# A gated graph network and a graph attention layer on one core: the weights of the beginning in a new order, two products of the end moved

## The chip, the cores and the metric

The kernel runs on one core of a Trainium2 chip. The metric is the device time of one execution in microseconds (us), lower is better. The core has five engines that run instruction streams of their own: TensorE (PE in the profile; its weight loads are listed apart as PEld), VectorE (DVE), ScalarE (ACT), GpSimd (POOL) and SyncE (SP). SyncE here only starts transfers; GpSimd starts those that add to what they find.

## The reference

The inputs are `x` (64 graphs, 256 nodes, 256 values, f32) and `adj` (64 x 256 x 256, zeros and ones, about one in 64 set). Two layers, each added to `x`:

```python
# layer 0: three steps of a gated graph network
h = relu(layernorm(x));  A = (adj != 0)
for l in range(3):
    m    = h @ weight[l]
    aggr = einsum('bst,bsd->btd', A, m)
    gi, gh = aggr @ w_ih.T + b_ih, h @ w_hh.T + b_hh       # 768 values each: r, z, n
    r = sigmoid(i_r + h_r); z = sigmoid(i_z + h_z)
    n = tanh(i_n + r * h_n)
    h = (1 - z) * n + z * h
x = x + h
# layer 1: graph attention, 4 heads of 64
v = relu(layernorm(x)) @ W.T + b
logits = leaky_relu(l_src[i] + l_dst[j], 0.2)              # l_src, l_dst: v times halves of a, per head
logits = where(adj == 1, logits, -9e15)
x = x + softmax(logits, over j) @ v
```

The message weights and the gates' input weights are multiplied into one another before use: the kernel needs `weight[l] @ w_ih.T` for each step, called `w_a[l]` here, with some sums and differences of its blocks.

## The kernel before

**Tiles.** The 64 graphs go through in 32 pairs, numbered 0 to 31. A pair has 512 nodes, four blocks of 128 rows. Layer 0 keeps the state turned (`hT_a`: values across partitions, nodes along the free axis), two halves of 512 elements; each graph of the pair is one half's inner part. A product of a step is a `block` (L302; its matmul is L313): four matmuls of 128x128 by 128x256 into one PSUM bank. The profile shows every f32 matmul as two, so a block as eight and the two small `pa` products of `value_weights` as four. The aggregation (`pa`, L470) works with the state in two parts, `hNhi` and `hNlo`, whose sum is the state and which are multiplied with `edge`, the adjacency as 0 and 1.

**Order.** Everything is entered in a plan: `at(tick, phase, p, fn)`. Ticks are run in order, the phases STEP, READY and REST within a tick, and of several pairs the later one first. The instructions are issued to the engines' streams in just that order (`tc.manual_schedule`), and each engine keeps it. Pair p starts at tick 18p. Its step l takes the ticks 12l to 12l+5 (`tick_0` to `tick_5`), `update` makes the new state in tick 12l+6, and the state is turned back to rows (`back`, PSUM bank `pback`) in ticks 12l+7 and 12l+8, where ScalarE copies `hNhi` (L798) and VectorE takes the difference `hNlo` (L799). Six ticks without a step follow each step; in them the next or the previous pair has a step of its own. So two pairs in different steps share TensorE, with the attention of earlier pairs between. Only at the two ends is there nothing to share with.

**Banks and buffers.** The steps' products have five PSUM banks of their own (`gate_bank`). All else, transposes and small products too, takes one of three banks in turn through `bank(name)`; a request waits until the bank's last reader is done. SBUF tiles have a tag with a fixed number of buffers: four of `zz` (logits later, weights as loaded at the beginning), two of `o`, two of `noedge`.

**The beginning.** Pair 0 has no neighbour, and its ticks 6 to 11 and 18 to 23 are partly filled with the weights, which are entered at the end of the program (L1018 to L1033):

- `biases` and `state_weights` at tick -5: the latter turns `w_hh` (banks `pw_hh`, copies to `hh_T` on ScalarE) and then issues six ScalarE operations for `w_n` and `w_h`. `state_weights_2` at -2 makes sums of them on VectorE.
- `first_hi` and `first_lo` of pair 0 (the two parts of its first state, L787 and after) at tick -3, `to_edge` (L764) at -2.5. The two halves of `hT_a` of pair 0 are turned at ticks -4 and -3.
- `input_weights` at tick 0 turns `w_ih` and the first message weights. `step_weights_T(l)` turns `weight[l]` (bank `pmT`), and ScalarE copies it to `w_msgT` (L232). `step_weights(l)` has four banks `pc_l` of two matmuls each, 128x128 by 128x384 (L239, four in the profile), copies each to `w_a[l]`, by VectorE and ScalarE in turn (L243), and after each two makes four sums S1, S2, S4 and -ZA of blocks on VectorE. The calls stand at ticks 0 and 1 for l = 0, 5 and 6 for l = 1, 13 and 14 for l = 2.
- `value_weights` at tick 20 prepares `w_val` (W turned, and behind it eight columns of W times the attention vectors) and `b_val`: a memset, then for each half two transposes (`pwv`, L280), a VectorE copy, two matmuls with 8 columns (`pwa`), a copy, and in the end the same for the bias (`bmat`, `pb`).

**Layer 1 of a pair.** From about tick 32 of the pair on: normalization, `values` (bank `pv`), `score_rows` (`as_rows`, L893: the scores are turned in bank `pscore`, written to DRAM as rows and read back for all partitions as `drow`), logits `zz` in which GpSimd's transfers add the score rows, maxima over the neighbours on VectorE (L949, reading `drow` and `noedge`), the shift `topT` written to DRAM and added to `zz` by GpSimd's transfers in the same way, exponentials (ScalarE), and for each block of rows `product` (bank `po`, 8 matmuls, 16 in the profile) with `divided`: VectorE's reciprocal `rden` and product `o` (L584), GpSimd's addition to `x` (L589). Pairs up to 28 enter a block's `output` at ticks 62 to 65 of the pair; for pairs below 29 (`dma_b`) `later` is six ticks, so that pair 28's last product stands at tick 71 of that pair.

**The end.** The last pair, 31, has its attention in `plan_tail` in a form without DRAM rows. From the end of its third step on, the order is a list written out by hand, `order` (L725), which mixes in what is left of pairs 29 and 30: `do("product", 2, r)` is the product of block r of pair 29, `do("rows", 1)` turns the maxima of pair 30 (`ptopT`, L887). The mask `noedge` of pair 31 is made by `bar` (L839 and around) at tick 28 of that pair.

Of the kernel before, what the change touches and what calls it, by code (L numbers as in the profile page):

```python
# [18 lines left out]
P = 128  # L19
# [8 lines left out]
def gated_gnn_then_gat_kernel(  # L28
# [51 lines left out]
    S0 = H * VC  # L80
    VW = S0 + 2 * H
    NPAIR = B // PB
# [15 lines left out]
    def bank(name):  # L98
        return ps_m.tile([P, 512], F32, tag="mm", name=name)
# [5 lines left out]
    def buf(tag, shape, name, dtype=F32):  # L105
        return sb.tile(shape, dtype, tag=tag, name=name, bufs=BUFS.get(tag, 1))
# [41 lines left out]
    w_nat = load_square("zz", "w_nat", W)  # L148
# [6 lines left out]
    ident = const.tile([P, P], F32, name="ident")  # L155
# [7 lines left out]
    for i in range(GB):  # L163
        pt = gate_bank(f"fill_{i}")
# [11 lines left out]
    def turn_gates(name, nat, dst, evict):  # L176
        for k in range(KD):
            for g0 in range(0, G, 3):
                pt = bank(f"pw_{name}_{k}_{g0}")
                for g in range(3):  # L180
                    nc.tensor.transpose(pt[:, ts(g, P)], nat[:, g0 + g, ts(k, P)], ident)
                evict[g0 // 3](dst[k][:, g0 * P : (g0 + 3) * P], pt[:, : 3 * P])
# [20 lines left out]
    RA, ZA, NA, S1, S2, S4 = range(6)  # L203
    def state_weights():
        turn_gates("hh", hh_nat, hh_T, (nc.scalar.copy, nc.scalar.copy))
        for k in range(KD):
            r_, z_, n_ = (hh_T[k][:, ts(g, D)] for g in range(3))
            nc.scalar.mul(w_n[:, (N00, N01)[k], :], n_[:, :P], 0.5)
            nc.scalar.mul(w_n[:, (NS3, N11)[k], :], n_[:, P:], 0.5)
            nc.scalar.copy(w_h[:, k, ts(RH, D)], r_)  # L210
# [13 lines left out]
    def step_weights_T(l):  # L224
        w_msgT[l] = buf("zz", [P, KD, D], f"w_msgT_{l}")
        pt = bank(f"pmT_{l}")
        for e in range(KD):
            for k in range(KD):
                nc.tensor.transpose(
                    pt[:, e * D + k * P : e * D + (k + 1) * P], w_msgs[l][:, k, ts(e, P)], ident  # L230
                )
        nc.scalar.copy(w_msgT[l].rearrange("q e d -> q (e d)"), pt)  # L232

    def step_weights(l):
        for k in range(KD):
            for g0 in range(0, G, 3):
                pt = bank(f"pc_{l}_{k}_{g0}")
                for e in range(KD):
                    nc.tensor.matmul(  # L239
                        pt[:, : 3 * P], w_msgT[l][:, e, ts(k, P)], ih_T[e][:, g0 * P : (g0 + 3) * P],  # L240
                        start=(e == 0), stop=(e == KD - 1),
                    )
                (nc.scalar.copy if g0 else nc.vector.tensor_copy)(  # L243
                    w_a[l][:, k, g0 * P : (g0 + 3) * P], pt[:, : 3 * P]
                )
            blk = [w_a[l][:, k, ts(j, D)] for j in range(6)]
            nc.vector.tensor_add(blk[S1], hh_T[k][:, D : 2 * D], blk[ZA])  # L247
            nc.vector.tensor_sub(blk[S2], blk[S1], hh_T[k][:, :D])
            nc.vector.tensor_sub(blk[S4], blk[RA], blk[S2])
            nc.vector.tensor_scalar_mul(blk[ZA], blk[ZA], -1.0)  # L250

    w_val = const.tile([P, KD, VW], F32, name="w_val")
    b_val = const.tile([P, VW], F32, name="b_val")

    a_exp = const.tile([P, KD, 2 * H], F32, name="a_exp")
# [5 lines left out]
    def load_vectors():  # L261
# [10 lines left out]
            bass.AP(tensor=b.tensor, offset=b.offset, ap=[[0, P], [C, H], [1, C]]),  # L272
        )

    def value_weights():
        nc.vector.memset(w_val, 0.0)
        for k in range(KD):
            pt = bank(f"pwv_{k}")
            for g in range(KD):
                nc.tensor.transpose(pt[:, ts(g, P)], w_nat[:, g, ts(k, P)], ident)  # L280
            nc.vector.tensor_copy(
                w_val[:, k, :S0].rearrange("q (h c) -> q h c", h=H)[:, :, :C],
                pt[:, :D].rearrange("q (h c) -> q h c", h=H),
            )
            pa = bank(f"pwa_{k}")
            for g in range(KD):
                nc.tensor.matmul(
                    pa[:, : 2 * H], w_nat[:, g, ts(k, P)], a_exp[:, g, :],
                    start=(g == 0), stop=(g == KD - 1),
                )  # L290
            nc.vector.tensor_copy(w_val[:, k, S0:], pa[:, : 2 * H])
        bmat = buf("o", [P, KD, P], "bmat")
        pb = bank("pb")
        for k in range(KD):
            nc.vector.tensor_copy(bmat[:, k, :], bcol[:, k : k + 1].to_broadcast([P, P]))
        for k in range(KD):
            nc.tensor.matmul(
                pb[:, : 2 * H], bmat[:, k, :], a_exp[:, k, :], start=(k == 0), stop=(k == KD - 1)
            )
        nc.vector.tensor_copy(b_val[:, S0:], pb[:, : 2 * H])  # L300


    def flat(y):
# [23 lines left out]
    def at(tick, phase, p, fn):  # L327
        plan.setdefault(tick, ([], [], []))[phase].append((-p, fn))
# [265 lines left out]
    def plan_tail(t0, p, v, g, turn_back, residual):  # L594
# [126 lines left out]
        def do(what, q, *key):  # L721
            return left[what, p - q, *key]

        at(t0 + 28, REST, p, links)
        order = (  # L725
            lambda: g.update(0), do("rows", 1), do("product", 2, 0), lambda: turn_back(0), lambda: g.update(1),
            do("product", 2, 1), lambda: residual(0), lambda: stats(0), do("add", 1), lambda: turn_back(1),
            do("product", 2, 2), lambda: residual(1), lambda: result(0), lambda: turned(0), lambda: stats(1),
            do("product", 2, 3), do("divided", 2, 0), lambda: values(0), lambda: result(1), lambda: turned(1),
# [11 lines left out]
    def plan_pair(p):  # L741
# [5 lines left out]
        def ready(t, fn):  # L747
            at(t0 + t, READY, p, fn)
# [4 lines left out]
        def rest(t, fn):  # L753
            at(t0 + t, REST, p, fn)
# [12 lines left out]
        dma_a = p >= 2  # L767
        norm_ticks = (-14, -13, -13, -10) if dma_a else (-14, -13, -13, -7)
        xn_a = plan_norm(lambda: v["x"], f"a{p}", p, [t0 + t for t in norm_ticks])
        ready(-1 if p else -2.5, to_edge)  # L770
        if dma_a:
            ready(-9.5, lambda: nc.scalar.activation(flat(xn_a["xn"]), flat(xn_a["xn"]), AF.Relu))
            h = plan_turn(lambda: xn_a["xn"], "hT_a", f"a{p}", p, [t0 - 9, t0 - 8, t0 - 3])
# [9 lines left out]
            hi, lo = map(flat, v["hN"])  # L783
            nc.vector.scalar_tensor_tensor(lo, flat(xn_a["xn"]), 0.0, hi, op0=ALU.max, op1=ALU.subtract)

        ready(-3, first_hi)
        rest(-3, first_lo)  # L787

        def back(l, i):

# [50 lines left out]
                nc.sync.dma_start(v["noedge_rows"].rearrange("r q t -> q r t"), v["noedge"])  # L841

        rest(16 if last else 22, load_adj_1)
        ready(28 if last else 35, bar)
        if last:
            plan_tail(t0, p, v, g, lambda i: turn_back(L - 1, i), residual)
            return
# [156 lines left out]
        if p >= NPAIR - 3:  # L1004
            for r in range(R):
                left["product", p, r] = lambda r=r: product(p, r, logits[r // KN], v, bank if late else gate_bank)
                left["divided", p, r] = lambda r=r: divided(p, r, v, nc.gpsimd.tensor_add)
            left["write", p] = lambda: write(p, v["x"], 0, R)
        else:
            for r, t in enumerate((62, 63, 64, 65)):  # L1010
                rest(t + later, output(r))
            rest(66 + later, lambda: write(p, v["x"], 0, R))

# [3 lines left out]

    at(-5, READY, 0, biases)  # L1018
    at(-5, REST, 0, state_weights)
    at(-2, READY, 0, state_weights_2)  # L1020

    def input_weights():
# [3 lines left out]
    at(0, REST, 0, input_weights)  # L1026
    at(1, REST, 0, lambda: step_weights(0))
    at(2, REST, 0, load_vectors)
    at(5, REST, 0, lambda: step_weights_T(1))
    at(SUB, REST, 0, lambda: step_weights(1))  # L1030
    at(13, REST, 0, lambda: step_weights_T(2))
    at(14, REST, 0, lambda: step_weights(2))
    at(20, REST, 0, value_weights)  # L1033
    for tick in sorted(plan):
        for phase in plan[tick]:
# [32 lines left out]
```

## Time and profile before

| quantity | value |
|---|---|
| median of three runs | 2495.89 us (2495.83 to 2496.14) |
| profiled execution, its own time | 2498.09 us |
| its span (first to last instruction) | 2496.3 us |
| mean granted TensorE clock | 0.997 of full |
| TensorE busy | 2464.2 us, 99% of the span |
| VectorE busy | 1992.2 us, 80% |
| ScalarE busy | 1437.5 us, 58% |
| GpSimd busy | 494.3 us, 20% |
| memory traffic (HBM) over the span | 109 GB/s |
| instructions | 37566 |
| chain that ended last, by engine | PE 83%, DVE 12%, ACT 3% |

Durations and busy times come from one profiled execution; it took 2.2 us more than the median of the runs without a profile, and its span is 1.8 us shorter than its own time. A line number such as L313 is a line of the kernel before. `out<-in` names the tiles that an instruction writes and reads. In a list of waits, `A L1 <- B L2: 2.8, 2, 1.5` says that instructions of tile A at line 1 were held up by those of tile B at line 2, for 2.8 us in all, 2 times, 1.5 us at most. The granted clock is the share of full speed at which TensorE ran. A busy share of 99% does not say that TensorE runs at its peak: a matmul counts as busy at a lower clock as well.

### The profile page before, as it was taken

The page shows a single profiled execution, that of the slowest core. Times are in us where ns is not written, and L with a number is a line of the kernel's source. Part 1 is how long each engine was busy: PE and PEld are TensorE (multiplying, and loading weights), DVE is VectorE, ACT ScalarE, POOL GpSimd, SP SyncE. Part 2 cuts the span into 40 slices and gives each one's busy share as a digit, 9 for nine tenths or more (in the row PEclk, how much of TensorE's full clock was granted, in tenths as well). Part 3 has the DMA queues.
Part 4 walks back from the last instruction along what each step waited for, and adds up shares of the span by engine and source line. Part 5 has one row for each costly group of instructions (what it writes and reads, how often), then busy time and mean ns, then how long its engine had stood idle before and what let it go on. Part 6 is the DMA issues. An engine that isn't in the chain of part 4 may idle for free.

```text
span 2496.3 us, 37566 instructions
## 1 busy us (share of the span) xinstructions
PE 2464.2 (99%) x13446; PEld 2191.9 (88%) x13446; DVE 1992.2 (80%) x4671; ACT 1437.5 (58%) x3007; POOL 494.3 (20%) x419
## 2 busy tenths in 40 slices
PE   8999999999999999999999999999999999999998
PEld 6888888888988888988888988888888889888887
DVE  5678877888877888777888778888778888778767
ACT  3445556555556555566565566565565555665664
POOL 0011121221221121212121212121212222212212
PEclk9999999999999999999999999999999999999999
DMA  3025656455656456656556565556565556564455
GB/s 95 9 68 119 152 119 153 121 127 134 136 127 155 119 126 143 132 131 147 116 131 148 117 146 138 116 130 147 122 153 127 123 132 140 125 157 118 107 109 110
DMA packets 322090, 313.72 MB, mean 126 GB/s; under 512 B 166560, under 2 KB 282224, under 8 KB 321904
## 3 DMA queue, kind: packets, MB, share of 16 engines
q0 software_dynamic: 33728, 130.03, 27.4%
q1 hardware_dynamic: 286608, 181.29, 27.0%
q8 instruction: 106, 1.74, 0.3%
q14 instruction: 80, 0.66, 0.1%
q10 hardware_dynamic: 1568, 0.01, 0.0%
HBM read 215.62 MB, written 56.60 MB: 109 GB/s over the span
## 4 chain that ended last, share of the span: by engine, by line
PE 83%; DVE 12%; ACT 3%; issue 1%; DMA 1%; POOL 0%; SPq 0%; ACTq 0%; DVEq 0%; POOLq 0%
PE pd L313 18%; PE pn L313 13%; PE pc L313 9%; PE po L573 8%; PE pe L313 7%; PE pa L470 5%; PE qb L448 5%; PE p L313 5%; PE pv L864 5%; PE qa L448 4%; PE pback L808 2%; DVE hT_a L559 2%; DVE any L949 2%; DVE R L558 2%; DVE hNlo L799 1%
## 5 line engine op out<-in xcount | busy, mean ns | idle before, releaser
L313 PE MATMUL pn<-aggr,w_a 128*128 128x256 f32 x1536 | 364.9, 380 | 2.8 <-DVE pn L526 2.8
L313 PE MATMUL pd<-T,w_a 128*128 128x256 f32 x1536 | 366.4, 382 | 0.0
L541 POOL TENSOR_TENSOR R<-hT_a,hn 128x512 f32<-128x512 f32 x96 | 141.9, 1479 | 1124.5 <-ACT hn L537 1042.5
L313 PEld LDWEIGHTS pn<-aggr,w_a 128*128 128x128 f32 x1536 | 286.9, 190 | 44.3 <-DVE pn L526 2.1
L313 PEld LDWEIGHTS pd<-T,w_a 128*128 128x128 f32 x1536 | 288.1, 191 | 37.6
L573 PEld LDWEIGHTS po<-val,zz 128*128 128x128 f32 x2048 | 244.9, 192 | 4.5
L537 ACT ACTIVATE hn<-pn,bi 128x256 f32<-128x256 f32 x384 | 160.4, 470 | 145.6 <-PE pn L313 145.4
L589 POOL TENSOR_TENSOR x<-x,o 128x256 f32<-128x256 f32 x124 | 137.1, 1107 | 538.3 <-DVE o L584 538.3
L558 DVE SCALAR_TENSOR_TENSOR R<-Z,R 128x512 f32<-128x512 f32 x192 | 132.5, 690 | 137.9 <-POOL R L541 126.3
L573 PE MATMUL po<-val,zz 128*128 128x65 f32 x2048 | 242.1, 272 | 0.0
L969 ACT ACTIVATE zz<-zz,val 128x256 f32<-128x256 f32 x496 | 223.7, 505 | 0.0
L949 DVE CUSTOM_DVE_ANT_0 any<-drow,noedge 128x256 f32<-128x256 f32 x496 | 209.1, 422 | 9.3 <-DMA drow<-score_dram 0.5
L455 ACT ACTIVATE R<-pc,brz 128x256 f32<-128x256 f32 x192 | 80.5, 470 | 230.8 <-PE pc L313 230.8
L526 DVE SCALAR_TENSOR_TENSOR pn<-R,hn 128x512 f32<-128x512 f32 x192 | 149.1, 777 | 77.3 <-ACT R L455 54.7
L455 ACT ACTIVATE R<-pe,brz 128x256 f32<-128x256 f32 x192 | 80.4, 470 | 213.5 <-PE pe L313 213.5
L313 PE MATMUL pd<-T,w_h 128*128 128x256 f32 x768 | 184.4, 383 | 3.1 <-DVE pe L510 0.4
L313 PE MATMUL pc<-aggr,w_a 128*128 128x256 f32 x768 | 182.5, 381 | 0.0
L313 PE MATMUL p<-T,w_a 128*128 128x256 f32 x768 | 181.9, 379 | 0.6 <-DVE w_a L247 0.6
L313 PE MATMUL pe<-aggr,w_a 128*128 128x256 f32 x768 | 181.4, 379 | 0.0
L313 PE MATMUL pc<-hT_a,w_h 128*128 128x256 f32 x768 | 181.4, 379 | 0.0
L799 DVE TENSOR_TENSOR hNlo<-pback,hNhi 128x512 fp32r<-128x512 f32 x128 | 88.2, 689 | 110.9 <-ACT hNhi L798 110.9
L313 PEld LDWEIGHTS pd<-T,w_h 128*128 128x128 f32 x768 | 143.5, 190 | 32.8 <-DVE pe L510 14.5
(183 smaller groups left out, 5323.0 us busy)
## 6 DMA issues: line engine op xcount, KB each, us to landing
zz<-score_dram POOLq DMA_DIRECT2D x62, 1024.0 KB, 11.0
zz<-topT_dram POOLq DMA_DIRECT2D x62, 1024.0 KB, 7.9
adj<-in_adj_dram SPq DMA_DIRECT2D x64, 512.0 KB
drow<-score_dram SPq DMA_DIRECT2D x62, 512.0 KB
x<-in_x_dram SPq DMA_DIRECT2D x32, 512.0 KB
out_dram<-x SPq DMA_DIRECT2D x31, 512.0 KB
words_dram_a<-words_a SPq DMA_DIRECT2D x30, 512.0 KB
words_dram_b<-words_b SPq DMA_DIRECT2D x29, 512.0 KB
```

Source lines behind the costliest of these rows:

```text
L313: nc.tensor.matmul(pt[:, ts(c, N)], w[:, k, j * D + c * P : j * D + (c + 1) * P], src[:, k, :], start=start and c == 0 and k == 0, stop=(c ...
L448: nc.tensor.matmul(pt, w_n[:, j, :], src, start=start, stop=True, skip_group_check=True)
L455: nc.scalar.activation(of(dst, i)[:, c, :], src[:, c, :], AF.Tanh, bias=brz[:, g0 + c : g0 + c + 1], scale=0.5)
L470: nc.tensor.matmul(pt[:, ts(i, N)], hN[half][:, i * KN + s, ts(e, P)], edge[:, i * KN + s, :], start=(s == 0 and half == 0), stop=(s == KN ...
L526: nc.vector.scalar_tensor_tensor(by_c(self.bank(f"pn{i}")), of(self.R, i), 1.0, of(self.hn, i), op0=ALU.add, op1=ALU.mult)
L537: nc.scalar.activation(n__[:, c, :], p_n[:, c, :], AF.Tanh, bias=bi[:, 2 * KD + c : 2 * KD + c + 1])
L541: nc.gpsimd.tensor_sub(of(self.R, i), of(self.hT(), i), n__)
L558: nc.vector.scalar_tensor_tensor(d_, of(self.Z, i), 1.0, d_, op0=ALU.add, op1=ALU.mult)
L573: nc.tensor.matmul(po[:, ts(h_, VC)], zz[:, j, h_, ts(s, P)], v["val"][:, i * KN + j, ts(h_, VC)], start=(j == 0), stop=(j == KN - 1),)
L589: add(v["x"][:, r, :], v["x"][:, r, :], o)
L949: nc.vector.tensor_tensor_reduce(any_, drow[r // KN][:, h, :], v["noedge"][:, r, :], 1.0, -3.0e38, ALU.add, ALU.max, accum_out=v["top"][:, ...
L969: nc.scalar.activation(zz[:, h, :], zz[:, h, :], AF.Prelu, alpha=ALPHA, bias=v["val"][:, r, S0 + H + h : S0 + H + h + 1],)
```

## The change

Six edits. In the beginning, `to_edge` and the two parts of pair 0's first state are entered at tick -4.5, and the six operations for `w_n` and `w_h` are split off as `state_weights_1` and entered at -2.5 (A). The message weights of steps 1 and 2 are turned at ticks 4 and 5, multiplied at 6 and 8, and their sums are split off as `step_sums` and entered at 8.5 and 13 (B). `value_weights` has all its transposes first, then all small matmuls in one bank, then the copies; the memset of `w_val` and the matrix `bmat` are made at tick 17 (C). At the end, the last product of pair 28 (`po_3`) is entered one tick later (D), `noedge` of pair 31 at tick 25 and not 28 (E), and in the list of the tail the first product of pair 29 stands before the rows of pair 30 (F).

```diff
     def state_weights():
         turn_gates("hh", hh_nat, hh_T, (nc.scalar.copy, nc.scalar.copy))
+
+    def state_weights_1():
         for k in range(KD):
             r_, z_, n_ = (hh_T[k][:, ts(g, D)] for g in range(3))
             nc.scalar.mul(w_n[:, (N00, N01)[k], :], n_[:, :P], 0.5)
...
+            if l == 0:
+                step_sums(l, k)
+
+    def step_sums(l, *ks):
+        for k in ks:
             blk = [w_a[l][:, k, ts(j, D)] for j in range(6)]
             nc.vector.tensor_add(blk[S1], hh_T[k][:, D : 2 * D], blk[ZA])
...
+    bmat = []
+
+    def bias_matrix():
+        nc.vector.memset(w_val, 0.0)
+        bmat.append(buf("o", [P, KD, P], "bmat"))
+        for k in range(KD):
+            nc.vector.tensor_copy(bmat[0][:, k, :], bcol[:, k : k + 1].to_broadcast([P, P]))
+
     def value_weights():
-        nc.vector.memset(w_val, 0.0)
+        pts = [bank(f"pwv_{k}") for k in range(KD)]
+        pa = bank("pwa")
         for k in range(KD):
-            pt = bank(f"pwv_{k}")
             for g in range(KD):
-                nc.tensor.transpose(pt[:, ts(g, P)], w_nat[:, g, ts(k, P)], ident)
+                nc.tensor.transpose(pts[k][:, ts(g, P)], w_nat[:, g, ts(k, P)], ident)
+        for k in range(KD):
+            for g in range(KD):
+                nc.tensor.matmul(
+                    pa[:, ts(k, 2 * H)], w_nat[:, g, ts(k, P)], a_exp[:, g, :],
+                    start=(k == 0 and g == 0), stop=(g == KD - 1), skip_group_check=True,
+                )
+        for k in range(KD):
+            nc.tensor.matmul(
+                pa[:, ts(KD, 2 * H)], bmat[0][:, k, :], a_exp[:, k, :],
+                start=False, stop=(k == KD - 1), skip_group_check=True,
+            )
+        for k in range(KD):
             nc.vector.tensor_copy(
...
-            lambda: g.update(0), do("rows", 1), do("product", 2, 0), lambda: turn_back(0), lambda: g.update(1),
+            lambda: g.update(0), do("product", 2, 0), do("rows", 1), lambda: turn_back(0), lambda: g.update(1),
...
-        ready(-1 if p else -2.5, to_edge)
+        ready(-1 if p else -4.5, to_edge)
...
-        ready(-3, first_hi)
-        rest(-3, first_lo)
+        ready(-3 if p else -4.5, first_hi)
+        rest(-3 if p else -4.5, first_lo)
...
-        ready(28 if last else 35, bar)
+        ready(25 if last else 35, bar)
...
-            for r, t in enumerate((62, 63, 64, 65)):
+            for r, t in enumerate((62, 63, 64, 66 if p == NPAIR - 4 else 65)):
                 rest(t + later, output(r))
...
+    at(-2.5, READY, 0, state_weights_1)
     at(-2, READY, 0, state_weights_2)
...
-    at(5, REST, 0, lambda: step_weights_T(1))
+    at(4, REST, 0, lambda: step_weights_T(1))
+    at(5, REST, 0, lambda: step_weights_T(2))
     at(SUB, REST, 0, lambda: step_weights(1))
-    at(13, REST, 0, lambda: step_weights_T(2))
-    at(14, REST, 0, lambda: step_weights(2))
+    at(8, REST, 0, lambda: step_weights(2))
+    at(8.5, REST, 0, lambda: step_sums(1, 0, 1))
+    at(13, REST, 0, lambda: step_sums(2, 0, 1))
+    at(17, REST, 0, bias_matrix)
     at(20, REST, 0, value_weights)
```

More of the change, by code (lines that the diff above doesn't have):

```diff
@@ L273, in load_vectors @@
         )
+    bmat = []
[4 more added lines that the diff above has]
+            nc.vector.tensor_copy(bmat[0][:, k, :], bcol[:, k : k + 1].to_broadcast([P, P]))
     def value_weights():
-        nc.vector.memset(w_val, 0.0)
+        pts = [bank(f"pwv_{k}") for k in range(KD)]
+        pa = bank("pwa")
         for k in range(KD):
-            pt = bank(f"pwv_{k}")
             for g in range(KD):
-                nc.tensor.transpose(pt[:, ts(g, P)], w_nat[:, g, ts(k, P)], ident)
+                nc.tensor.transpose(pts[k][:, ts(g, P)], w_nat[:, g, ts(k, P)], ident)
[11 more added lines that the diff above has]
+        for k in range(KD):
             nc.vector.tensor_copy(
                 w_val[:, k, :S0].rearrange("q (h c) -> q h c", h=H)[:, :, :C],
-                pt[:, :D].rearrange("q (h c) -> q h c", h=H),
+                pts[k][:, :D].rearrange("q (h c) -> q h c", h=H),
             )
[L285 to L300, printed above, removed]
+            nc.vector.tensor_copy(w_val[:, k, S0:], pa[:, ts(k, 2 * H)])
+        nc.vector.tensor_copy(b_val[:, S0:], pa[:, ts(KD, 2 * H)])
     def flat(y):
```

## The prediction

> **What bounds the kernel now.** I read the page first, then TensorE's list of waits, then the order of time around each wait, the granted clock in slices of 1 us, and the chain that ended last.
>
> The page's first part says how much there is to win:
>
> ```profile
> PE 2464.2 (99%) x13446; PEld 2191.9 (88%) x13446; DVE 1992.2 (80%) x4671; ACT 1437.5 (58%) x3007; POOL 494.3 (20%) x419
> ```
>
> TensorE idles 2496.3 - 2464.2 = 32.1 us; the list says where (total, times, longest):
>
> ```profile
> PE pn L313 <- DVE pn L526: 2.8, 2, 1.5
> PE pa L470 <- DVE edge L764: 2.2, 1, 2.2
> PE pback L808 <- DVE hT_a L559: 2.2, 1, 2.2
> ...
> PE ptopT L887 <- DVE top L960: 1.5, 1, 1.5
> PE pwv L280 <- DVE hNlo L799: 1.3, 1, 1.3
> PE pa L470 <- DVE hNlo L799: 1.3, 1, 1.3
> PE pc L239 <- ACT w_msgT L232: 1.0, 1, 1.0
> ```
>
> All but the first lie in the first 100 us or the last 90, where the change works. After some of them TensorE is also slow (slice, engines' busy time, then granted clock, DMA share, GB/s):
>
> ```profile
> 16.00:17.00 1.00, 1.00 (x5) 1.00 (x6) 0.96 (x6) 0.00 (x0) 0.00 (x0) 0.56 1.10 330
> ...
> 95.00:96.00 1.00, 1.00 (x5) 1.00 (x6) 0.07 (x1) 0.00 (x0) 0.00 (x0) 0.50 0.00 0
> ```
>
> The order of time shows the price; the same block of eight takes 1.73 us from start to next start elsewhere, here 3.55 and 2.79:
>
> ```profile
> 95.75 3.76 PE L313 MATMUL pd<-T,w_a 128*128 128x256 f32 x8
> 99.30 2.96 PE L313 MATMUL pc<-aggr,w_a 128*128 128x256 f32 x8
> 102.09 0.59 PE L448 MATMUL qb<-T4n,w_n 128*128 128x256 f32 x2
> ```
>
> The chain in the last 90 us runs through two transfers, then VectorE's maxima:
>
> ```profile
> 2427.55 0.30 SPq L893
> 2427.90 5.21 DMA score_dram<-score
> 2433.17 4.33 DMA drow<-score_dram
> 2437.52 0.42 DVE any L949
> ```
>
> [...]half rate 2419.1 to 2422.5 after 2.35 us idle, and 94.6 to 101.5[...]; but 1.76 us idle at 2447.85 halved nothing. [...]so a waiting rden_3 holds up everything behind it (its 5.03 us wait at 2416.43 agrees). [...]the score writes land 5.2 us after issue while POOL's topT adds run, and the reads that wait for them were issued only 1.7 us after the first write at 2357.76, with no adds running.
>
> **A, beginning.** ScalarE now makes hNhi before both hT_a halves and the six w_n/w_h operations. After the last hh_T copy (11.05): hNhi 0.95, to 12.05; two hT_a 0.50 each, to 13.05; six operations 1.4, to 14.45. VectorE makes edge at 10.6, when the biases are done, and hNlo at 12.1 to 13.3. qa needs the first w_n: 13.35 (13.08 before). pa can follow at 13.8 instead of 15.98, and takes 1.91 at full clock (as at 82.54) instead of 3.43: it ends at 15.7, not 19.41. New wait: the w_n sums start at 14.2, behind ScalarE's operations, take 1.74 and T 0.68, so the second qa starts at 16.7. Gain 19.4 - 16.7 = 2.7. Bounds: 1.2 if pa still runs at half clock (16 x (213 - 119) ns = 1.5 less), 3.0 if the sums are quicker.
>
> **B, step weights.** Before, 45.59 to 57.77 (12.18 us) holds 9.24 of work (pmT 0.44, pc 5.16, pback 0.87, qa 0.43, pa 1.91, qa 0.43): 2.94 is lost. Now pmT of step 1 goes before pn, pmT of step 2 behind it, and the second pc (5.16) between pback and qa. Both copies of w_msgT and hNlo are covered by a pc. But the eight sums of w_a (1.46 per half) stand on VectorE before T. From the end of pn: the third bank of the second pc is there at 0.44 + 5.16 + 0.87 + 3.87 = 10.34, copied by 11.0; sums to 13.9; T by 14.6, T2n by 15.3. TensorE reaches the second qa at 13.97 and waits 0.65, then 0.27 for T2n. Gain 2.94 - 0.92 = 2.0; bounds 1.0 (sums slower by 1) and 2.9. The second set of sums, 2.9 us behind T2, ends about 4 us before its users; that cover gone, T4n would be late next.
>
> **C, value weights.** Before, 90.77 to 102.09 is 11.32 us: four transposes 0.44, twelve small matmuls 1.4, pd and pc 3.46, together 5.3; the rest waiting and half clock. Now the transposes come together, the twelve matmuls follow with no VectorE step between, and w_val's memset and bmat are made at tick 17. There they add 0.51 + 0.7 us before pair 0's update, which leaves 1.9 us idle before hNlo: hidden. One wait stays: with three banks in turn, pwa gets the one that pback_1 used, so it waits for hNlo, done at 92.73, from 91.2: 1.5 us. Time 5.3 + 1.5 = 6.8; gain 4.5. Unknown is the clock. Waiting and small matmuls make 2.9 us in a row[...], where there were 4.8. I take full clock; one window at half rate costs 1.7, two 2.9. Bounds 1.6 and 4.5.
>
> **D, po_3 of pair 28 one tick later.** VectorE's rden_3 no longer stands before the updates, nor pt_b behind po_3. Update 0 needs the Z half (2413.37) and POOL (2413.04), so hT_a is ready at 2414.8 instead of 2418.87; TensorE goes from po_3 (2416.7) to pback, waits 0.65 for ScalarE's hT_b (2417.65, unmoved), and stays at full clock. VectorE then does hNlo 2419.65, four val additions, score 2422.8: pscore at 2422.8 instead of 2426.2, gain 3.4. What follows it is a transfer. POOL's additions of x and its topT adds move 0.75 later behind o_3, to 2422.3 to 2433.7 on the rings. The score write, issued at 2424.1, lands at 2429.7 (5.6 as now), but the drow read then meets the second topT add: it can start at about 2433 and land at 2436.2, against 2437.2. Of 3.4 I keep 1.0. Bounds: -0.5 (it waits for all topT) and 3.4. ScalarE's exps of pair 29 now come 2.5 us before their topT data; R and hn behind them are still ready by 2437.4, before TensorE's pn at 2438.8.
>
> **E, noedge at tick 25.** 0.60 us of VectorE leaves the maxima's row (2441.42) for an idle stretch of 2.2 us at 2432: gain 0.6, and plink's wait of 0.4 is within it.
>
> **F, po_0 before ptopT.** It fills the 1.5 us wait, but pback next waits for hT_a, which VectorE sets: 0. It saves 1.2 only if VectorE is not the chain; a loss is excluded, as topT's copy stands behind hT_a anyway.
>
> No other instruction moves; the orders of SP and POOL are unchanged, and the pairs between keep TensorE's chain, so the early gain passes through. Sum: 2.7 + 2.0 + 4.5 + 1.0 + 0.6 = 10.8 us. The profiled execution took 2498.09 (span 2496.3), so 2487.3; the median of the three runs is 2.20 lower: 2495.89 - 10.8 = 2485.1.
>
> **Rivals.** (1) The clock still falls at the value weights: C gives 1.6 to 2.8 and not 4.5, taking 2.2: 8.5 us, 2487.4. For it: pwa's wait is left, and 128x8 matmuls may not count as busy[...]. (2) The score write and drow wait for all of topT: D gives -0.5 and not 1.0: 9.3 us, 2486.6. For it: the writes' packets ended within 0.1 us of topT's[...]. (3) The drow read gets its turn at once: D gives 3.4: 13.2 us, 2482.7. Against it speak the 5.2 us of the score write. (4) Slower: topT's adds still fill POOL's queue when the score adds (2 MB, 10.4 us on the rings at their measured pace from 2439.3) join it, and drow gets no turn until both are through: 2433.7 + 10.4 + about 6 = 2450 instead of 2437.2, 12.8 lost where 1.0 was counted: 10.8 - 13.8 = -3.0, 2498.9. It decides if drow lands after 2447; past 2452 it shows as slower. Against: now drow is served first, though score adds are issued 0.5 us behind it.
>
> **How the numbers follow.** Main case 0.46, clock 0.25, topT in the way 0.16, drow at once 0.09, slower 0.04. 0.2%, 5.0 us, is about what can be told from no change. The first four cases give 8.5 to 13.2, and a clock loss with topT in the way 7.0; 2482.0 to 2489.0 leaves out under 2 in 10. Faster by over 0.2%: 0.89; within: 0.07 (B at its lower bound with both losses, or the fourth rival as priced); slower: 0.04.
>
> **What would show it.** pa at 119 ns and a second qa near 16.7; no wait for w_msgT, and one of 0.6 for T; value weights with one wait of 1.5 and no 0.50 in the clock after it; the 2.2 of pback gone; pscore at 3.4 more than the early gain, drow only 1. Wrong if pd and pc again take over 2 us each, if drow lands after today's place, or if a wait on ScalarE's exps appears.

## The result

| | before | after |
|---|---|---|
| median of the executions | 2498.06 us (2495.78 to 2505.44, 12) | 2490.82 us (2488.08 to 2498.14, 12) |
| profiled execution, its own time | 2498.09 us | 2489.74 us |
| its span | 2496.3 us | 2488.0 us |

The ratio is 0.9973 with a 95% interval of 0.9964 to 0.9982: between 4.5 and 9.0 us are gained. Forecast were 10.8 us and 2485.1 us in a range up to 2489.0. The direction was right; the time lies above the range. Executions of one kernel differ in steps, and their mean granted clock with them: of 63 later executions of before, seven took 2495.6 to 2496.5 us (clock 0.999), 44 took 2497.2 to 2499.2 (0.997 or 0.998) and twelve about 2505 (0.993 or 0.994; none of these was profiled, and what they hold is open). The three on which the forecast was based (median 2495.89) fell among the fastest, which was luck; 2.2 us of the miss are that base.

Both profiled executions can be compared place by place. All times are starts on TensorE, except the maximum, which is on VectorE:

| place | before | after | gain so far | part | forecast |
|---|---|---|---|---|---|
| second `qa` of pair 0's first step | 19.41 | 16.94 | 2.47 | A 2.5 | 2.7 |
| `qa` of pair 1's first step | 81.94 | 77.60 | 4.34 | B 1.9 | 2.0 |
| `qb<-T4n` behind the value weights | 102.09 | 95.04 | 7.05 | C 2.7 | 4.5 |
| last pair, second step, `pd` by `w_h` | 2403.53 | 2396.45 | 7.08 | pairs between 0 | 0 |
| `pscore` | 2426.21 | 2415.91 | 10.30 | | +3.4 |
| first maximum behind `drow` | 2437.52 | 2429.13 | 8.39 | D 1.3 | 1.0 |
| `pt_b` of the last pair | 2456.49 | 2447.16 | 9.33 | D, E, F 2.25 | 1.6 |
| last `po` group | 2481.20 | 2472.86 | 8.34 | end: -1.0 | 0 |

The fourth row is used as the anchor of the tail below. The first part of the page of after:

```profile
PE 2460.8 (99%) x13446; PEld 2194.2 (88%) x13446; DVE 1990.9 (80%) x4671; ACT 1437.7 (58%) x3007; POOL 493.8 (20%) x419
```

TensorE idles 27.2 us, 4.9 less than before, although the span is 8.3 shorter: the rest, 3.4 us, is TensorE's busy time, which has shrunk because less of it ran at half clock (7.7 us of the span against 15.8, by the record of the granted clock). The list of TensorE's waits of after (total, times, longest):

```profile
PE pn L326 <- DVE pn L539: 4.8, 4, 1.5
...
PE pwa L298 <- issue: 1.5, 1, 1.5
...
PE pt_b L649 <- DVE xn_b L640: 0.9, 1, 0.9
PE qa L461 <- DVE T L447: 0.9, 1, 0.9
...
PE qa L461 <- ACT aggr L487: 0.6, 1, 0.6
...
PE pback L822 <- DVE hT_a L572: 0.2, 1, 0.2
```

The waits for `edge`, `hNlo`, `w_msgT` and `noedge` are gone, that of `pback` fell from 2.2 to 0.2, and the value weights have one wait of 1.5 as expected. New is 2 us more of waiting for `pn`, in the tail. Then the order of time at the value weights, and the granted clock there and in the tail (engines' busy time, granted clock, DMA share, GB/s):

```profile
86.42 0.60 PE L295 MATMUL pwv<-ident,w_nat 128*128 128x128 f32 x4
88.48 1.04 PE L298 MATMUL pwa<-a_exp,w_nat 128*128 128x8 f32 x8 [1.46 <-issue]
89.37 0.59 PE L303 MATMUL pwa<-a_exp,bmat 128*128 128x8 f32 x4
89.82 2.66 PE L326 MATMUL pd<-T,w_a 128*128 128x256 f32 x8
92.27 2.93 PE L326 MATMUL pc<-aggr,w_a 128*128 128x256 f32 x8
95.04 0.60 PE L461 MATMUL qb<-T4n,w_n 128*128 128x256 f32 x2
```

```profile
91.00:92.00 1.00, 1.00 (x4) 0.82 (x3) 0.00 (x0) 0.00 (x0) 0.00 (x0) 0.50 0.00 0
...
2448.00:2449.00 1.00, 1.00 (x12) 1.00 (x11) 0.90 (x6) 0.60 (x1) 1.00 (x2) 1.00 0.50 70
2450.00:2451.00 1.00, 1.00 (x3) 0.78 (x3) 1.00 (x3) 0.00 (x0) 0.52 (x1) 0.50 1.07 213
```

`pd` and `pc` take 2.45 and 2.77 from start to next start where 1.73 was counted: the clock is at half rate from 90.96 to 94.37 us, one stretch of 3.41 us, where before had 6.83 us in a row (94.62 to 101.45). A second stretch of 3.41 us, from 2449.57 to 2452.98, is new and takes back part of the tail's gain. Last, the chain in the tail:

```profile
2417.25 0.30 SPq L907
2417.55 0.05 issue
2417.60 6.01 DMA score_dram<-score
...
2423.67 5.44 DMA drow<-score_dram
2429.11 0.02 issue
2429.13 0.43 DVE any L963
```

It still runs through the two transfers, which now take 11.5 us together against 9.5 before: of the 3.2 us by which `pscore` came earlier, 1.9 were lost there.

### The profile page after: what moved, and what is told of

The parts are those of the page before. It is cut to its first block, busy times and chain, and to the rows that moved or that the text cites. A ratio compares the mean times of both kernels' runs of the same rounds, so it can differ in the third digit from the quotient of the medians.

```text
span 2488.0 us, 37565 instructions
## 1 busy us (share of the span) xinstructions
PE 2460.8 (99%) x13446; PEld 2194.2 (88%) x13446; DVE 1990.9 (80%) x4671; ACT 1437.7 (58%) x3007; POOL 493.8 (20%) x419
## 4 chain that ended last, share of the span: by engine, by line
PE 83%; DVE 13%; ACT 3%; issue 1%; DMA 1%; SPq 0%; POOL 0%; ACTq 0%; DVEq 0%; POOLq 0%
PE pd L326 18%; PE pn L326 13%; PE pc L326 9%; PE po L586 9%; PE pe L326 7%; PE pa L483 5%; PE qb L461 5%; PE p L326 5%; PE pv L878 5%; PE qa L461 4%; PE pback L822 2%; DVE hT_a L572 2%; DVE R L571 2%; DVE any L963 2%; DVE hNlo L813 1%; ACT zz L983 1%
```

## The experiments

The author's assumption from here on, called share: half rate follows where TensorE streams few columns, whether or not it has an instruction. The rival, called idle, is the reading on which the forecast was built: only idle time counts. By a window at half rate, or a slow window, the forecast and the expectations mean a stretch at half rate like the two of after, 3.41 us each; the 0.67 in the second expectation is the author's estimate of how often one follows the value weights.

### Value weights: the wait, the small matmuls and the clock

First the changed kernel again, beside the three that follow.

> The changed kernel itself, on the chip of the next three. Theory (share): [...]So the times of one kernel should differ from execution to execution by steps of about 1.7 us, with the clock in step. Median about 2490.8 us, T4n's matmul of pair 0's step 2 (value weights' landmark) at 95.0 us with a slow window and at 93.3 without. Rival (idle): only time without any instruction counts; then pd and pc behind the gap are slow for another reason and are slow every time.

Measured: median 2489.79 us (2489.60 to 2490.60), ratio 0.9964 (0.9951 to 0.9977). The block from `pwv` to `qb<-T4n` takes 8.62 us again, with a half-rate stretch from 90.7 to 94.1 us and one from 2449.3 to 2452.7. The five executions lay within 1 us, so no steps of 1.7 us were seen in them. They were seen in the profiles: of the eight kernels profiled with this wait unchanged, five took 8.62 to 8.64 us for the block and three (A undone, E undone, and the one without `topT`'s transfers) 6.93 to 6.98. So a cause that makes `pd` and `pc` slow every time is out.

Next, both halves of `pwv` in one bank:

```diff
-        pts = [bank(f"pwv_{k}") for k in range(KD)]
+        pwv = bank("pwv")
+        pts = [pwv[:, ts(k, D)] for k in range(KD)]
```

> Both pwv halves in one bank, so that pwa takes a bank whose reader is long done. Theory (share): the wait of 1.46 us goes, what is left of the gap is 1.35 us of 128x8 matmuls[...]: pd and pc take 1.73 each from start to start, T4n's matmul at 95.0 - 1.5 - 1.8 = 91.8 us, median 1.5 + 0.67 x 1.7 = 2.6 us below the changed kernel. Rival (the small matmuls themselves slow what follows, whatever waits): T4n at 93.6, 1.5 us below.

The order of time of this kernel:

```profile
87.16 0.60 PE L296 MATMUL pwv<-ident,w_nat 128*128 128x128 f32 x4
87.60 0.96 PE L299 MATMUL pwa<-a_exp,w_nat 128*128 128x8 f32 x8
88.41 0.59 PE L304 MATMUL pwa<-a_exp,bmat 128*128 128x8 f32 x4
88.86 1.97 PE L327 MATMUL pd<-T,w_a 128*128 128x256 f32 x8
90.67 1.89 PE L327 MATMUL pc<-aggr,w_a 128*128 128x256 f32 x8
92.39 0.59 PE L462 MATMUL qb<-T4n,w_n 128*128 128x256 f32 x2
```

No wait, no half rate, and the block takes 5.23 us instead of 8.62 (its start varies by up to 1.1 us with the clock at the beginning, see the last section, so lengths are compared). Of the 3.39 saved, 1.62 are the wait (`pwa` starts 0.44 behind `pwv` and not 2.06), the other 1.77 the clock. Median 2485.98 us (2484.51 to 2494.69), ratio to before 0.9952 (0.9937 to 0.9968): 3.8 us below the changed kernel beside it, more than the 2.6 expected; in the profiles it is 3.6 of span (2488.0 and 2484.4), with both of the changed kernel's half-rate stretches gone. That of the tail went by luck, since nothing in the tail was changed: it is worth about 1.0, and the later start took 0.7 back. The full clock behind the small matmuls is not that of one profile alone: in all five kernels profiled with one bank and the small matmuls issued once, the granted clock stays at 1.00 over this block. This kernel is faster than before and than the changed kernel.

Then the wait kept, but filled with columns that nobody reads:

```diff
+        for j in range(12):
+            nc.tensor.transpose(pts[j % KD][:, D + (j // KD % 2) * P : D + (j // KD % 2 + 1) * P], ident, ident)
```

> Twelve more transposes of the identity (1.3 us) into unused columns of the pwv banks, in the wait before pwa; the wait's time stays. Theory (share): TensorE streams through the wait[...], pd and pc at full clock: T4n's matmul at 95.0 - 1.8 = 93.3 us, median about 1.1 us below the changed kernel. Rival (the wait for the bank is what costs, and the slow pd and pc come from VectorE or the banks): T4n at 95.0, no gain.

```profile
86.58 1.47 PE L297 MATMUL pwv<-ident 128*128 128x128 f32 x12
88.20 1.04 PE L300 MATMUL pwa<-a_exp,w_nat 128*128 128x8 f32 x8
89.10 0.59 PE L305 MATMUL pwa<-a_exp,bmat 128*128 128x8 f32 x4
89.54 1.97 PE L328 MATMUL pd<-T,w_a 128*128 128x256 f32 x8
91.35 1.89 PE L328 MATMUL pc<-aggr,w_a 128*128 128x256 f32 x8
93.08 0.59 PE L463 MATMUL qb<-T4n,w_n 128*128 128x256 f32 x2
```

`pwa` starts as late as before (2.06 us behind the first `pwv`), but `pd` and `pc` run at full clock: 6.94 us for the block (from the first `pwv`, at 86.14), 1.68 less. So here the bank's wait, filled, did not slow what follows. That agrees with share, but does not show it alone, as three of the eight profiles with the wait unfilled had full clock too. The median of 2489.08 us (0.9961, 0.9949 to 0.9973) is only 0.7 below the changed kernel's: this profile had two half-rate stretches in the tail, in a row from 2445.95 to 2452.78.

The case that parts share from idle: no wait, TensorE always with an instruction, but the twelve 128x8 matmuls issued three times.

```diff
+        for again in range(2):
+            for k in range(KD):
+                for g in range(KD):
+                    nc.tensor.matmul(
+                        pa[:, ts(8 + k, 2 * H)], w_nat[:, g, ts(k, P)], a_exp[:, g, :],
...
+                nc.tensor.matmul(
+                    pa[:, ts(10, 2 * H)], bmat[0][:, k, :], a_exp[:, k, :],
```

> As the one before the last (both pwv halves in one bank), with the twelve 128x8 matmuls issued three times (the first two sets into columns that nobody reads): 24 more of about 112 ns, 2.7 us. TensorE has an instruction all the time. Theory (share): 4.0 us in a row stream almost nothing[...]: T4n's matmul at 91.8 + 2.7 + 1.7 = 96.2 us, up to 97.4. Rival (idle): no idle time, full clock, T4n at 94.5 us.

```profile
89.27 1.04 PE L311 MATMUL pwa<-a_exp,w_nat 128*128 128x8 f32 x8
90.16 0.59 PE L316 MATMUL pwa<-a_exp,bmat 128*128 128x8 f32 x4
90.61 3.42 PE L339 MATMUL pd<-T,w_a 128*128 128x256 f32 x8
93.83 2.17 PE L339 MATMUL pc<-aggr,w_a 128*128 128x256 f32 x8
```

There is no idle time before `pd`, and yet it runs at half rate from 90.97 on, for 3.41 us. The block takes 9.60 us, 4.37 more than in one bank: 24 x 0.111 = 2.67 for the matmuls, and 1.70 for the clock. Idle time alone does not explain this half rate; that few columns were streamed agrees with it. Median 2492.08 us (0.997, 0.9958 to 0.9982).

### The beginning

A undone (`edge`, the halves and `state_weights_1` in their old places):

> The changed kernel with edge, the first halves and the w_n/w_h operations in their old order. Theory: pa waits 2.2 us for edge[...], so that pa runs at half clock: the second qa starts at 19.4 us (16.9 with A), and all of the 2.5 us is there at the anchor of the tail (2398.9 for 2396.4). Rival (a part is caught up in the first steps): less than 2 us at the anchor.

TensorE's waits of this kernel up to 25 us show the one that A took away:

```profile
PE pa L482 <- DVE edge L776: 2.2, 1, 2.2
```

The clock falls to half from 15.9 to 19.3 us, and the second `qa` starts at 19.49 (16.94 with A). At the anchor only 0.6 us of it are seen, 2397.05 against 2396.45, which looks like the rival. But in this execution the value weights ran at full rate (6.93 us for the block, not 8.62): the second `qa` of pair 1 still starts 2.47 later (82.41 and 79.94), and less the 1.69 by which the block is shorter, `qb<-T4n` 0.79 later. The last 0.2 up to the anchor lie within what the stretch from there to the anchor varies by from profile to profile (2301.0 to 2301.4 us), of which no cause was looked for. So A's gain passes through the first steps; what differs is the clock at the value weights. Median 2493.88 us (0.998, 0.997 to 0.999), 3.1 above the changed kernel's, though the two intervals overlap.

B undone (the step weights' calls and sums in their old places):

> The changed kernel with the step weights in their old places and their sums inline. Theory: waits for w_msgT (1.0) and for hNlo (1.3) come back, the first matmul of pair 1 (qa at 77.6 us in the changed kernel) starts 1.9 us later, and so does the anchor of the tail (2398.3 for 2396.4), with the value weights' own gap as it is. Rival: the clock falls in the gap before pa, and 3 us or more are lost.

```profile
PE pa L482 <- DVE hNlo L812: 1.2, 1, 1.2
PE pc L241 <- ACT w_msgT L234: 1.0, 1, 1.0
```

Both waits are back, the granted clock stays at 1.00 there, and the anchor is at 2398.42, 1.97 later, with the value weights' block alike (8.64). Not all of it is B: the second `qa` of pair 0's first step, ahead of what B moves, starts 0.49 later already, because the clock was released later at the beginning (16.8 us against 12.5, see the last section). From there to the first `qa` of pair 1 (79.90 and 77.60) B is worth 1.81. Median 2491.69 us (0.9973, 0.9964 to 0.9982), not to be told from the changed kernel's.

### The tail

D undone, `(62, 63, 64, 65)` for all pairs:

> The changed kernel with pair 28's po_3 back at its old tick. Times from the anchor, the last pair's second-step pd by w_h near 2396.5 us. Theory: pback again waits 2.2 us, pscore comes at anchor + 22.7 us (19.5 with D), the first maximum (drow landed) at + 34.0 (32.7), since most of D's 3.2 us is lost to the transfers; the last po starts 1.3 us later than with D or, if TensorE stays at full clock in the window before pv (which it did not in the changed kernel), hardly later. Rival (E and F made the tail's gain): no loss at the end.

`pback` waits 2.18 us again, `pscore` comes at anchor + 22.69, the first maximum at + 34.20 (32.68 with D): D is worth 3.2 at `pscore` and 1.5 behind the transfers. The last `po` starts 3.5 us later than in the changed kernel, against 1.3 expected, since two half-rate stretches in a row, 2449.5 to 2456.3, fell into this execution. Median 2490.72 us (0.9968, 0.9956 to 0.998), no different from the changed kernel's in the executions.

What holds the transfers up was tested by leaving out the two that add `topT` to pair 29's logits:

```diff
-            rest(56 + later, add_rows(0, "topT"))
-            rest(57 + later, add_rows(1, "topT"))
+            if p != NPAIR - 3:
+                rest(56 + later, add_rows(0, "topT"))
+                rest(57 + later, add_rows(1, "topT"))
```

> The changed kernel without the two transfers that add topT to pair 29's logits (that pair's softmax is left without its shift, so its output is not the reference's). Theory: these 2 MB on the rings hold up pair 30's score write (6.0 us after issue) and drow's read (5.4); without them the write takes about 2 us and the read about 4, drow is there before VectorE is ready for it, the first maximum comes at anchor + 30.3 instead of 32.7 and the end is 2.0 to 2.4 us earlier. Rival (drow's 1 MB to all partitions is slow by itself): first maximum at 32 or later, end within 0.7.

VectorE in order of time:

```profile
2424.75 0.70 DVE L523 TENSOR_TENSOR pe<-pd,m 128x512 f32<-128x512 f32 x1 [0.85 <-PE pd L326]
2425.36 0.41 DVE L963 CUSTOM_DVE_ANT_0 any<-drow,noedge 128x256 f32<-128x256 f32 x1
```

The maximum follows directly, without a wait for `drow`, at anchor + 30.13. The score write's last packet ended 1.9 us after its issue, against 7.0 in the changed kernel. So `topT`'s 2 MB are the cause, and they cost 2.5 us at this place; the last `po` starts at anchor + 73.74, 2.0 earlier than in one bank, whose tail had no half-rate stretch either. Median 2486.66 us (0.9952, 0.9936 to 0.9967).

E undone:

> The changed kernel with noedge of pair 31 back at tick 28. Theory: VectorE is the chain from drow to the last pair's normalization; noedge takes 0.6 us out of the middle of its row of maxima, so xn_b and pt_b come 0.6 us later from the anchor (50.7 in the changed kernel). Rival (TensorE's own waits for pn hide it): pt_b unmoved within 0.1.

```profile
2432.66 0.62 PE L620 MATMUL plink<-ident,noedge 128*128 128x128 bf16 x8 [2.27 <-DVE noedge L852]
2433.12 2.96 PE L326 MATMUL pn<-aggr,w_a 128*128 128x256 f32 x8
2435.87 2.61 PE L326 MATMUL pd<-T,w_a 128*128 128x256 f32 x8
```

`pt_b` comes at anchor + 52.43, 1.7 later than in the changed kernel, not 0.6. With D in place `plink` reaches `noedge` earlier than before and would wait 2.27 us for it, not 0.38, and behind this wait the clock is at half rate from 2433.9 to 2437.3 us, within `pn` and `pd`. How much of the 1.7 is VectorE's 0.6 and how much the clock, this execution does not part. Median 2489.24 us (0.9961, 0.9946 to 0.9976), not to be told from the changed kernel's.

F undone:

> The changed kernel with the rows of pair 30 ahead of pair 29's first product again. Theory (F is worth 0): TensorE waits about 0.5 us for the maxima's top, po_0 and pback_0 follow 0.4 later, but VectorE is the chain and its hT_a of the second half moves by less than 0.2 us; pt_b at anchor + 50.7 within 0.2. Rival (F saves TensorE's wait, 1.2): pt_b 1.2 later.

Measured: `pt_b` at anchor + 50.55 (50.71), the last `po` at + 75.26 (76.41), median 2488.25 us (0.9955, 0.994 to 0.997). The first 0.16 hints at a loss by F, the rest is the clock, which did not fall in the tail here. To part them, F was undone in the one-bank kernel, whose tail stayed at full clock:

```diff
-            lambda: g.update(0), do("product", 2, 0), do("rows", 1), lambda: turn_back(0), lambda: g.update(1),
+            lambda: g.update(0), do("rows", 1), do("product", 2, 0), lambda: turn_back(0), lambda: g.update(1),
```

> One bank for pwv, and the tail's order without F. Theory (F costs: VectorE, the chain there, waits for ptopT behind po_0): pt_b at anchor + 50.5 (51.0 in one_bank), the last po at anchor + 75.3 (75.7), median 0.4 below one_bank's 2486.0 less what the chips differ. Rival (F is worth 0 or a gain, and the changed kernel lost by its slow window alone): pt_b at 51.0 or later.

`pt_b` at anchor + 50.82 (51.04 with F), the last `po` at + 75.52 (75.74): F costs 0.2 us, half of what was expected; in the median, 2485.84 us (0.9951, 0.9937 to 0.9964), it can't be told. There is a second effect of F in the profiles: with it TensorE waits 0.87 us for the first `pt_b`, without it 0.46, with `po` on both sides. Of the ten profiles with the wait of 0.86 to 0.87 us, six have half rate that begins within 2.5 us of this `pt_b` (2449.57 in the changed kernel, whose `pt_b` is at 2447.16); of the four with 0.46 us (before among them) none has. That points to F as what opened this place to half rate, without showing it; in the medians of 2485.98 and 2485.84 us nothing of it is seen. Where the 0.2 us go is seen on VectorE in the changed kernel:

```profile
2440.57 0.69 DVE L572 SCALAR_TENSOR_TENSOR hT_a<-R,hn 128x512 f32<-128x512 f32 x1
2441.45 0.28 DVE L903 COPY topT<-ptopT 16x128 f32<-16x128 f32 x1 [0.18 <-PE ptopT L901]
2441.66 0.67 DVE L570 TENSOR_TENSOR R<-hT_a,hn 128x512 f32<-128x512 f32 x1
```

The copy of `topT` stands between the two halves' updates and now waits for `ptopT`, which TensorE issues only after `po_0`.

Then an attempt to use what was found: the first of pair 29's two `topT` transfers issued three ticks earlier, F undone, one bank.

```diff
-            rest(56 + later, add_rows(0, "topT"))
+            rest(53 if p == NPAIR - 3 else 56 + later, add_rows(0, "topT"))
```

> Both pwv halves in one bank, the tail's order without F, and the first of pair 29's two topT transfers issued three ticks earlier (its rows are in DRAM at 2402.4 us and GpSimd is idle then), so that only 1 MB of them is left when pair 30's scores are written. Theory (the topT transfers set when drow lands): the first maximum comes at anchor + 30.1 to 31.3 instead of 32.8, the last po at anchor + 73.4 to 74.4 instead of 75.7; median 1.5 to 2.5 us below that of one_bank, 2483.5 to 2484.5 us. Rival (one transfer of 1 MB holds the queue as long as two): first maximum at 32.5 or later, and only F's 0.5 us is gained.

It was a miss: `pscore` fell back to anchor + 22.61, the first maximum to + 34.49, the last `po` to + 78.09; median 2487.66 us (0.9958, 0.9944 to 0.9971). The chain shows the new collision:

```profile
2403.43 8.39 DMA link<-noedge_dram
2411.84 1.06 ACT zz L937
```

The earlier transfer meets the read of pair 30's mask, whose packets take from 2407.9 to 2411.3 us beside those of `topT` (2403.9 to 2410.5), where in the changed kernel they take 1.2 us. ScalarE waits 3.9 us for that mask, `hNhi` of the last pair stands behind it on ScalarE, and the third step starts late. Moved away from one neighbour, the transfer has run into another.

Last, transposes that nobody reads in TensorE's wait before the last pair's `pt_b`, with this change and in the one-bank kernel:

```diff
+            if i == 0:
+                for j in range(6):
+                    nc.tensor.transpose(pt[:, ts(j % 4, P)], ident, ident)
```

> The same with six transposes of the identity (0.65 us) ahead of the last pair's first pt_b, where TensorE waits 0.5 to 0.9 us for xn_b[...]. Theory (share): no slow window in the tail in any execution, spread smaller, highest times nearer to the lowest; the median equal or up to 0.7 us below the same kernel without them, and above it by 0.2 us at most where they outlast the wait. Rival (the steps of time come from something else than these windows): same spread.

> One bank for pwv, F as in the changed kernel, and six transposes of the identity (0.65 us) in the wait of 0.87 us before the last pair's first pt_b. Theory (share of streamed columns): no slow window near 2450 us in any execution[...]; the times of the executions lie closer together than one_bank's (2484.5 to 2486.5), pt_b's own transposes unmoved. Rival (the windows come from elsewhere): as spread as before.

With the earlier transfer: median 2488.07 us (0.9958, 0.9946 to 0.9971; 2487.74 to 2488.84), the last `po` at anchor + 78.24; the one half-rate stretch was that of the late third step, 2417.2 to 2420.6. In the one-bank kernel: 2486.03 us (0.9955, 0.9943 to 0.9968; 2485.49 to 2489.63), the last `po` at + 76.17, no half-rate stretch. The profiles show none near 2450 us in either, but the times did not lie closer together than without, and neither median is better. Whether the filling pays stays open; the one-bank kernel without it had no half-rate stretch in its profile either, and the kernel with the earlier transfer, which is without F, had none near 2450 us before it was filled.

## Why the prediction was right and where it was wrong

**A and B.** Right, each 0.1 to 0.2 us too high. The wait for the second `qa` was 0.85 us where 0.9 follows from the working; TensorE's 0.6 us before T in pair 0's second step came as a wait for `aggr` with T done beside it, and the 0.27 for T2n did not come. That `pa` ran at full clock was in part luck: in seven of the 14 profiles of kernels with A the clock was released only at 16.8 to 17.7 us, and the second `qa` started at 17.4 to 17.8, not at 16.7 to 16.9. Both profiles compared here had the early release.

**C.** Wrong, and this is the step that failed: "Waiting and small matmuls make 2.9 us in a row", and behind it, "I take full clock." The 2.9 us were right (86.86 to 89.82), and so was the one wait of 1.5. But that 2.9 us in a row would leave the clock full was shown by no trace of before. Of eight profiles with this wait, five had half rate behind it. In the other three the block took 6.93 to 6.98 us, near the forecast's 6.8, and a gain of 4.4; so full clock was possible, but it was taken as given. The prediction's example for it, 1.76 us idle at 2447.85 in before that halved nothing, is one place in one profile: in after 0.87 us idle ahead of 2447.16, between products with 65 columns, was followed by half rate. The first rival had it: it priced C between 1.6 and 2.8, and C measured 2.7 (read from one profile of each kernel; no run undoes C alone). Its reason, that 128x8 matmuls may not count as busy, agrees with the kernel with three sets of them, which had half rate without idle time.

**D.** Right in kind. `pscore` gained 3.2 (forecast 3.4), and of that the transfers left 1.3 (forecast 1.0), since `topT`'s additions held them up; the landing of `drow` was forecast at 2436.2 on before's time and came at 2429.1 + 7.1. The rivals that drow is served at once, that it waits for all of `topT`'s additions at a loss, or that it queues behind the score's, fell: its first packet starts at 2425.5 us, the last of `topT` ends at 2426.0, so it did wait for them, but with a gain of 1.3 left. Without `topT`'s two transfers the read is at once.

**E** was put at 0.6; undone, it costs 1.7 at `pt_b` in one profile, a half-rate stretch included that is not parted from it, as with D `plink` would have waited 2.3 us and not 0.4. The interaction was not looked for.

**F** was put at 0 with "a loss is excluded, as topT's copy stands behind hT_a anyway". It stands behind the first half's `hT_a` and ahead of the second half's R, so it can wait, and what waits behind it is the chain: 0.2 us lost.

**The tail's sum** was 1.6; at `pt_b` it was 2.25. Then the new half-rate stretch took 1.0, of which nothing was foreseen: the forecast asked where the change makes TensorE idle longer, and here the wait of 0.87 us (0.46 before) lies between products (`po`) that stream 65 columns in 0.108 us, where a transpose streams 128 in 0.109. That longer wait is F's, by the profiles with and without it.

**The sum.** In the profiles 10.8 was forecast and 8.34 measured: C 1.8, the tail 0.3, A and B 0.3. From the forecast's base, 2495.89, to the median of twelve, 2498.06, are another 2.2; the last 1.1 is the difference between the profiled execution of after and its kernel's median, which no profile explains (a late release of the clock at the beginning would be of that size; that it is the cause is not shown).

## What to carry to other kernels

A gap on TensorE cost its length here and, where a stretch of 3.41 us at half rate followed, about 1.7 us more (8.62 us for the value weights against 6.93). Three sets of matmuls with 8 columns brought the 1.7 us without a gap, so count columns as well as instructions: here 8 columns took 0.112 us and 256 took 0.216. One profile at full clock does not show that a stretch is safe: with the same wait at the value weights three of eight profiles had full clock and five had not, and a difference of 1 to 2 us between two single profiles can be just that. A wait for a PSUM bank in rotation was removed here by packing two small results into one bank, which saved 3.4 us in the profile, 1.6 of the wait and 1.8 of the clock. A transfer moved away from one neighbour on the rings has to be followed to the next one (there the mask's packets took 3.4 us and not 1.2), and an edit that opens room (D) changes what its neighbours (E) are worth (a wait of 2.27 us for `noedge`, not 0.38).

## What the runs showed of the hardware

**Half rate.** In the records of the granted clock of before and after, each stretch at half rate from the first change of the clock to 2480 us lasts 3.41 or 6.83 us. In the slices of 1 us of the other kernels, the stretches seen whole last 3.4 or 6.8 us. This is how long TensorE was busy in the 3.41 us ahead of these five and of one in small_three, and with what:

| kernel | 3.41 us ahead | busy | what lies there | half rate behind it |
|---|---|---|---|---|
| before | 12.70 to 16.11 | 0.83 us | a wait of 2.20 us for `edge` | 3.41 us |
| before | 91.21 to 94.62 | 1.34 us | the value weights' waits and small matmuls | 6.83 us |
| before | 2415.68 to 2419.10 | 1.24 us | a wait of 2.18 us for `hT_a` | 3.41 us |
| after | 87.54 to 90.96 | 2.48 us | most of the wait of 1.46 us, twelve matmuls with 8 columns | 3.41 us |
| after | 2446.15 to 2449.57 | 2.48 us | a wait of 0.87 us, `po` with 65 columns | 3.41 us |
| small_three | 87.57 to 90.98 | all | no wait, matmuls with 8 columns up to 90.61 | 3.41 us |

Being busy does not keep the clock full: in small_three TensorE was busy all of the 3.41 us. The columns streamed are an estimate of the author's, from the pace of f32 matmuls in the trace of after (256 columns in 0.216 us, 128 in 0.109): in the last three rows 0.33, 0.37 and 0.14 of what TensorE would have streamed at that pace; in the one-bank kernel's block, which kept full clock, at least 0.62 in any 3.41 us. That agrees with share. What decides the clock, and how few columns are too few, these runs do not show.

**The beginning.** The kernels start at half rate, which the record of the granted clock does not show, since it begins with the first change (12.45 us in after); the mean clocks given leave it out. The pace shows it: of the 128x128 f32 transposes in

```profile
8.61 2.18 PE L181 MATMUL pw_hh<-ident,hh_nat 128*128 128x128 f32 x9 [0.96 <-DMA hh_nat<-in_L_gnn_w_hh_dram]
17.45 1.61 PE L181 MATMUL pw_ih<-ident,ih_nat 128*128 128x128 f32 x12
```

the first start 0.213 us apart, the second 0.109. The release comes at 11.4 to 12.7 us in nine profiles and at 16.8 to 17.7 in the other seven, whose value weights begin 0.5 to 1.1 us later where A and B are in place; what sets its time is not shown.

**A product with 65 columns** takes 0.108 us (16 in 1.73), as long as a 128x128 transpose (0.109): about half the columns in the same time.
